# Linear attention gated by an FP4 FFN on one core: w_down's quantization, block 0's Q, GpSimd's sums and the last FFN product at other places

## The chip, the cores and the metric

The kernel runs on one core of a Trainium2 chip. The metric is the device time of one execution in microseconds (us); lower is better. Shown are the median of three runs and the span of one profiled execution, which is what the profile's rows are measured against.

## The reference

Input x is 4 sequences of 2048 tokens with D = 256 features, float32. After a layer norm the tokens go through two branches, and the second gates the first:

```python
xn = _layernorm(x)
# branch 1: linear attention (16 heads of 64), then a GELU FFN of 1024
Q = elu(xn @ Wq + bq) + 1; K = elu(xn @ Wk + bk) + 1; v = xn @ Wv + bv
KV = einsum('bshd,bshm->bhdm', K, v)
Z = 1 / (einsum('bshd,bhd->bsh', Q, K.sum(axis=1)) + 1e-6)
o = einsum('bshd,bhdm,bsh->bshm', Q, KV, Z).reshape(b, s, 1024)
x1 = _layer_norm(xn + o @ Wo + bo, g1, be1)
s = _layer_norm(x1 + gelu(x1 @ W1 + b1) @ W2 + b2, g2, be2)
# branch 2: an FFN of 704 whose inputs and weights are rounded to FP4 (E2M1) in blocks of 16
h = silu(fp4(xn) @ fp4(w_gate).T) * (fp4(xn) @ fp4(w_up).T)
g = silu(fp4(h) @ fp4(w_down).T)
out = x + s * g
```

fp4 divides each block of 16 by its largest magnitude over 6, rounds to the grid 0, 0.5, 1, 1.5, 2, 3, 4, 6, and multiplies back.

## The kernel before

**Tiling.** Tokens go in blocks of 256 (TB = 2 tiles of 128), 8 blocks to a sequence, 32 blocks in all (n = 0 to 31). Matrix products are float32; each shows as two passes (two matmul instructions) in the trace. TensorE's results go to PSUM: 4 banks of the tag mm, 2 of acc and 2 of pxk.

**Stages.** First the keys of sequence 0, in a loop of 8 rounds (n = 0 to 7): pk is the key product, ek its Exp on ScalarE, kk the elu on VectorE, pxk the sum of kk against xn. Beside them the weights are loaded, and w_gate and w_up are quantized to FP4 by quantize_gu, two chunks a round in rounds 0 to 5, in three steps (scale and division; rounding and multiplication back; transposes on TensorE, pwgu, and copies by ScalarE). Then block 0's FP4 FFN (pg is gate and up, pd the down product), and the matrix M of each half of the heads: xk copied out of PSUM, pkv, kv copied, pm (kv times Wo), in four steps of m_of_half; m_sums on GpSimd then forms the weight sums for a product in seven parts.

The main loop over blocks runs, for block n: q_of (pq, its Exp e, the elu zq), the keys of the next sequence (two subs to a block: pk, kk, pxk), sums (pz, then 1/z, stored to DRAM as z_d and read back spread over rows as zb), the FP4 values of h (qT, a product of a spread scale and a transposed grid gridT, both fetched by DMA), gate_up of block n + 1 (pg), down (pd and g), qz (zq times zb), attention (pa, added to xn, then statistics and normalization to x1), ffn_2 of block n - 1 (py), the transposes of x1 (pt_x), the scales and grids of the coming blocks, output of block n - 1 (s, o, the store), ffn_1 (pf, Gelu to hT). Block 31 has nothing beside it, and its ffn_2 runs last.

**Products in seven parts.** ffn_2, and attention for sequences 0 to 2, split both operands in halves and get from seven half-by-half products what eight give in a plain one: seven_sums makes four sums of the left operand on VectorE, w2_sums (lines 219 to 222) and m_sums (601 to 604) four of the weights on GpSimd, and add_seven puts the parts together in five VectorE additions.

**What sets the order.** Matmuls and transposes stay in program order on TensorE. VectorE and ScalarE operations do as well until in_order[0] is set to False, behind the first M products; from there a list scheduler places them by priority, with tc.issue_after as a floor. GpSimd's long operations are chained by hand through pool["last"]: gate_addend (lines 801 to 803: o = g * be2 + x, g = g * g2), ffn_addend (809, 810), attention_addend (675), and the rstd power of stats (430). Nearly all DMAs go through SyncE's queue in order. A tile's next buffer waits for its readers: x has one buffer, zq, hT, w_down and the first rows share two of tag big.

down_steps holds the two generators of quantize_down (one for each 128 rows of w_down); in block 0 their first two steps run behind the quantized x, the third (six transposes pwd, three copies) ahead of down(0, 0).

Of the kernel before, what the change touches and what calls it, by code (L numbers as in the profile page):

```python
# [22 lines left out]
def linear_attention_gated_by_fp4_ffn(  # L23
# [396 lines left out]
    def stats(x, name, js=range(TB)):  # L420

        j0, j1 = js[0], js[-1] + 1
        mv = small.tile([P, TB, 2], F32, tag="mv", name=f"mv_{name}")
        rstd = small.tile([P, TB], F32, tag="rstd", name=f"rstd_{name}")
        for j in js:
            st = small.tile([P, 6], F32, tag="st", name=f"st_{name}_{j}")
            vector.bn_stats(st, x[:, j, :])
            vector.bn_aggr(mv[:, j, :], st)
        vector.tensor_scalar(rstd[:, j0:j1], mv[:, j0:j1, 1], LN_EPS, None, ALU.add)
        pool["last"] = nc.gpsimd.tensor_tensor(  # L430
            rstd[:, j0:j1], rstd[:, j0:j1], neg_half[:, j0:j1], ALU.pow
        ).ins
        return mv, rstd
# [343 lines left out]
    def down(n, j):  # L777
        if j == 0:
            blk[n]["pd"] = acc_tile(f"pd_{n}").rearrange("p (j d) -> p j d", j=TB)
        pd = blk[n]["pd"]  # L780
        for i in range(NI):
            mm(
                pd[:, j, :], qT[:, i, j * P : (j + 1) * P], wd[:, i, :], start=i == 0, stop=i == NI - 1
            )
        if j < TB - 1:
            return
        g = work.tile([P, TB, D], F32, tag="g", name=f"g_{n}")
        scalar.activation(g, pd, AF.Silu)

        o = work.tile([P, TB, D], F32, tag="o", name=f"o_{n}")  # L790
        x = work.tile([P, TB, D], F32, tag="x", name=f"x_{n}", bufs=1)
        nc.sync.dma_start(x, rows_of(src, n))
        blk[n]["g"], blk[n]["o"], blk[n]["x"] = g, o, x

    def gate_addend(n):
        g, o, x = (blk[n][k] for k in ("g", "o", "x"))
# [10 lines left out]
            pool["last"] = nc.gpsimd.tensor_tensor(x1, x1, rows["shift"], ALU.add).ins  # L810


    def q_of(n, first=None):

        xnT = blk[n].pop("xnT")
        zq = work.tile([P, NH, T], F32, tag="big", name=f"zq_{n}")
        blk[n]["zq"] = zq
        behind = None
        for cc in range(0, NH, 2):
            pq = mm_tile(f"pq_{n}_{cc}").rearrange("p (c t) -> p c t", c=2)  # L820
            e = work.tile([P, 2, T], F32, tag="e", name=f"e_{n}_{cc}", bufs=3)
            for ci in range(2):
                c = cc + ci
                for d in range(ND):
                    mm(
                        pq[:, ci, :], wq_sb[:, d, c * P : (c + 1) * P], xnT[:, d, :],
                        start=d == 0, stop=d == ND - 1,
                    )
            scalar.activation(e, pq, AF.Exp, bias=neg_one)
            if first is not None and cc == 0:  # L830
                behind = first()
            with tc.issue_after(behind.ins) if behind is not None else nullcontext():
                vector.scalar_tensor_tensor(zq[:, cc : cc + 2, :], e, 1.0, pq, ALU.min, ALU.max)
# [93 lines left out]
    def attention(n):  # L927
        x1 = work.tile([P, TB, D], F32, tag="x1", name=f"x1_{n}")
        xn = blk[n].pop("xn")
        b = n // NB  # L930
        if in_seven(b):
            pa = [acc_tile(f"pa0_{n}"), mm_tile(f"pa1_{n}")]
            seven_products(
                pa, blk[n].pop("zs"), lambda q: m_sb[b][q], (1, 2, 4, 3, 5, 7, 6), 0, 7 * FOUR
            )
            add_seven(x1, xn, pa)
        else:
            zq = blk[n].pop("zq")
            pa = acc_tile(f"pa_{n}").rearrange("p (j d) -> p j d", j=TB)
            for j in range(TB):  # L940
                for c in range(NH):
                    mm(
                        pa[:, j, :], zq[:, c, j * P : (j + 1) * P],
                        m_sb[b, c // FOUR][:, c % FOUR, :], start=c == 0, stop=c == NH - 1,
                    )
            vector.tensor_tensor(x1, xn, pa, ALU.add)
        mv, rstd = stats(x1, f"1_{n}")
        normalize(x1, x1, mv, rstd)
        blk[n]["x1"] = x1

    def x1_T(n):
        x1 = blk[n]["x1"]
# [50 lines left out]
        seven_products(blk[n]["py"], left, w2, order, lo, to)  # L1003

    def output(n):
        g, o, x1, py = (blk[n][k] for k in ("g", "o", "x1", "py"))
        s = work.tile([P, TB, D], F32, tag="s", name=f"s_{n}", bufs=1)

        add_seven(s, x1, py)
        mv, rstd = stats(s, f"2_{n}")  # L1010
        for j in range(TB):
            vector.scalar_tensor_tensor(
                s[:, j, :], s[:, j, :], mv[:, j, 0:1], g[:, j, :], ALU.subtract, ALU.mult
            )
        for j in range(TB):
            vector.scalar_tensor_tensor(
                o[:, j, :], s[:, j, :], rstd[:, j : j + 1], o[:, j, :], ALU.mult, ALU.add
            )
        nc.sync.dma_start(rows_of(out, n), o)


    def step(gen, times=1):
# [17 lines left out]
    for n in range(NB):  # L1040
        more = n + 1 < NB
        tiles = [(f, j) for f in range(2) for j in range(TB)]
        k, kk = {}, {}

        def product(i):
            k[i] = key_product(xnT, *tiles[i], f"0_{n}_{tiles[i][0]}")

        def elu(i):
            f, j = tiles[i]
            kk[i], _ = key_elu(*k[i], f"0_{n}_{f}_{j}")  # L1050

        def onto_xn(i):
            f, j = tiles[i]
            key_xk(0, f, xn, j, kk[i], n == 0 and j == 0, not more and j == TB - 1)

        product(0)
        if more:
            st = keys_stats(n + 1)
        product(1)
        elu(0)  # L1060
        product(2)
        dep = kk[0]
        elu(1)
        if more:
            xn_next = keys_norm(n + 1, *st)
        elu(2)
        onto_xn(0)
        product(3)
        if 2 * n < 2 * I // P:
            weight = quantize_gu(range(2 * n, min(2 * n + 2, 2 * I // P)))  # L1070
        step(weight)
        for load in later.get(n, ()):
            load(dep)
        onto_xn(1)
        step(ready)
        if n < 2:
            step(constants)
        onto_xn(2)
        elu(3)
        if not more:  # L1080
            quantized_x(-1)
        if more:
            xnT = keys_xnT(n + 1, xn_next)
        step(weight)
        onto_xn(3)
        ready = weight
        if n == 5:
            add_b2(dep)
            w_down_sb = load_down()
        if n == 6:  # L1090
            load_xn(0)
            scales_x(0)
            spread_scales(-1, False, True)
            grid_of_x(0)
            grid_T(-1, NI * TB, NCH * TB)
            m_0 = m_of_half(0, 0, dep, ahead=True)
            step(m_0)
        if more:
            xn = xn_next
    load_xn(1)  # L1100
    load_xnT(0)
    down_steps = [quantize_down(w_down_sb, k) for k in range(ND)]

    step(gate, 4)
    step(m_0)
    scales_h(0, 0)
    scales_x(1)
    step(gate, 4)
    scales_h(0, 1)
    m_half = m_of_half(0, 1)  # L1110
    step(m_half)
    step(m_0, 3)
    spread_scales(0, True, True)
    in_order[0] = False
    for sub in range(2):
        keys_in(1, sub)
# [22 lines left out]
    for n in range(NBLK):  # L1139
        b, bi = divmod(n, NB)  # L1140
        subs = (2 * bi, 2 * bi + 1) if b + 1 < B else ()
        if n < last:
            gate = gate_up(n + 1)
        if n > 0:
            gate_addend(n - 1)
        if subs:
            if n > 0:
                step(m_half)
            q_of(n)
            if n == 0:  # L1150
                for sub in subs:
                    keys_T(b + 1, sub)
            load_xnT(n + 1)
            kk_ins = keys_k(b + 1, subs[0])
            block_addends(n)
            if n == 0:
                with tc.issue_after(pool["last"]):
                    w2_sums()
            with tc.issue_after(kk_ins):
                ins = quantized_x(n)  # L1160
            with tc.issue_after(sums(n, ins.ins).ins):
                for j in range(TB):
                    quantized_h(n, j)
            with tc.issue_after(ins.ins):
                for g in down_steps if n == 0 else ():
                    step(g, 2)
            if n > 0:
                keys_T(b + 1, subs[1], keys["exp"])
            step(m_half)
            keys_xk(b + 1, subs[0])  # L1170
            step(gate, 9)
            step(m_half)
            for g in down_steps if n == 0 else ():
                step(g)
            down(n, 0)
            down(n, 1)
        elif n < last:
# [28 lines left out]
        if n > 0:  # L1206
            with tc.issue_after(kk_ins):
                ffn_sums(n - 1)
            attention(n)
        if n + 2 < NBLK:  # L1210
            load_xn(n + 2)
        if subs:
# [43 lines left out]
            output(n - 1)  # L1256
        if n + 1 == last:
            q_of(last)
            ffn_1(n, range(NF // 2))
            sums(last)  # L1260
            ffn_1(n, range(NF // 2, NF))
        else:
            ffn_1(n)
        for sub in next_subs[:1]:
            keys_T(bn + 1, sub, blk[n]["gelu"])
    ffn_2(last, 4)
    ffn_sums(last)
    ffn_2(last, 28, (1, 7, 2, 4, 5, 3, 6))
    output(last)


# [32 lines left out]
```

## Time and profile before

| | us |
|---|---|
| median of three runs (lowest, highest) | 1896.48 (1895.70, 1897.93) |
| the profiled execution | 1898.94 |
| its span | 1897.2 |
| TensorE's granted clock, mean of the span | 0.996 |
| ScalarE busy, of which table loads | 706.7, 156.5 |
| DMA traffic | 187.73 MB, 99 GB/s |

Block by block: pf of block 2 starts at 316.0 us in the span and pf of block 3 at 373.8; block 30's pf starts at 1844.0, block 31's at 1875.5, and the last matmul ends at 1888.9.

An excerpt line of the views has the start, the time taken, the engine, the line and operation, the tile written and those read, and in brackets the idle time before and who ended it. L103 and L106 are the helpers that issue matmuls and transposes, L119 the one that issues VectorE and ScalarE operations, so groups are told apart by their tiles. Names ending in q (SPq, DVEq) are an engine's queue.

### The profile page before, as it was taken

The numbers are of one execution on the slowest core, as the hardware profiler recorded it, in microseconds if no ns is written. First come the engines' busy times: TensorE is split into PE (matmuls) and PEld (weight loads), VectorE is DVE, ScalarE is ACT, GpSimd is POOL, SyncE is SP. The second block draws the span as 40 slices with busy tenths as digits, with TensorE's granted clock in tenths as the row PEclk, the third lists the DMA queues.
The fourth block names the chain that finished last, engine by engine and source line by source line (L and its number), as shares of the span: only waits on it lengthen the run. The fifth ranks groups of instructions, "written<-read, shape, count | busy, mean of one in ns | idle before, by whom it ended". The sixth has DMA issues, their size and how long they took to land.

```text
span 1897.2 us, 25223 instructions
## 1 busy us (share of the span) xinstructions
PE 1864.5 (98%) x9348; PEld 1385.3 (73%) x9348; DVE 1396.8 (74%) x2530; ACT 706.7 (37%) x1191; POOL 384.0 (20%) x360
## 2 busy tenths in 40 slices
PE   9999999999999999999999999999999999999997
PEld 4456577777777777777777777777787778888876
DVE  5658777766777777777677787775777768888875
ACT  2333444334334344443233443354333333333322
POOL 1412222011121212220112230222110122222211
PEclk9999999999999999999999999999999999999999
DMA  5525655454434456644344654465442344445531
GB/s 181 191 78 112 119 105 96 108 109 89 97 66 89 113 109 121 140 74 101 83 88 78 121 99 102 92 138 105 86 89 70 70 78 87 84 89 92 91 78 43
DMA packets 228250, 187.73 MB, mean 99 GB/s; under 512 B 107655, under 2 KB 189843, under 8 KB 228126
## 3 DMA queue, kind: packets, MB, share of 16 engines
q1 hardware_dynamic: 227292, 184.53, 47.2%
q8 instruction: 74, 1.21, 0.3%
q10 hardware_dynamic: 834, 1.58, 0.3%
q14 instruction: 50, 0.41, 0.1%
HBM read 130.91 MB, written 32.59 MB: 86 GB/s over the span
## 4 chain that ended last, share of the span: by engine, by line
PE 81%; DVE 9%; DMA 6%; issue 2%; POOL 1%; ACT 1%; SPq 0%; ACTq 0%; POOLq 0%; DVEq 0%
PE pg L103 14%; PE pq L103 10%; PE pk L103 10%; PE pxk L103 10%; PE pa L103 9%; PE pf L103 9%; PE pd L103 8%; PE py L103 7%; PE pz L103 2%; POOL rstd L430 1%; DMA xn_d<-xn_k 1%; DVE x L119 1%; DMA zb<-z_d 1%; DMA xn<-xn_d 1%; DVE scale L119 1%
## 5 line engine op out<-in xcount | busy, mean ns | idle before, releaser
L430 POOL TENSOR_TENSOR rstd<-rstd,neg_half 128x2 f32<-128x2 f32 x96 | 76.8, 801 | 1352.2 <-DVE rstd L119 1039.2
L103 PE MATMUL pg<-wgu,qT 128*128 128x352 f32 x1024 | 309.2, 460 | 0.0
L103 PEld LDWEIGHTS pg<-wgu,qT 128*128 128x128 f32 x1024 | 193.8, 190 | 116.7 <-issue 14.0
L103 PE MATMUL pf<-x1T,w_sb 128*128 128x256 f32 x1024 | 229.4, 382 | 5.1 <-DVE zq L119 2.7
L103 PE MATMUL pk<-wk_sb,xnT_k 128*128 128x512 f32 x512 | 230.7, 593 | 0.8 <-ACT xnT_k L119 0.7
L103 PE MATMUL pq<-xnT,wq_sb 128*128 128x256 f32 x1024 | 226.6, 379 | 3.3 <-ACT hT L119 3.3
L103 PE MATMUL pxk<-kk,xn_k 128*128 128x512 f32 x496 | 227.6, 598 | 1.8 <-DVE kk L119 1.8
L103 PEld LDWEIGHTS pf<-x1T,w_sb 128*128 128x128 f32 x1024 | 192.8, 191 | 32.8 <-DVE zq L119 3.1
L103 PEld LDWEIGHTS pq<-xnT,wq_sb 128*128 128x128 f32 x1024 | 194.2, 190 | 30.7 <-ACT hT L119 4.4
L103 PE MATMUL pd<-wd,qT 128*128 128x256 f32 x768 | 175.2, 384 | 1.5 <-DVE qT L119 1.3
L103 PEld LDWEIGHTS pk<-wk_sb,xnT_k 128*128 128x128 f32 x512 | 96.8, 190 | 103.0 <-issue 94.5
L119 ACT ACT_TABLE_LOAD x122 | 156.5, 1283 | 40.7 <-PE pk L103 25.8
L103 PEld LDWEIGHTS pd<-wd,qT 128*128 128x128 f32 x768 | 146.9, 192 | 28.1 <-DVE qT L119 3.5
L119 ACT ACTIVATE x1T<-pt_x,bcol 128x256 f32<-128x256 f32 x64 | 32.7, 561 | 357.4 <-PE pt_x L106 357.4
L103 PEld LDWEIGHTS pxk<-kk,xn_k 128*128 128x128 f32 x496 | 89.5, 190 | 100.4 <-issue 87.0
L119 DVE SCALAR_TENSOR_TENSOR kk<-ek,pk 128x512 f32<-128x512 f32 x128 | 85.7, 685 | 99.1 <-ACT ek L119 99.1
L119 DVE TENSOR_TENSOR h<-h,pg 128x352 f32<-128x352 f32 x128 | 66.1, 516 | 100.3 <-PE pg L103 98.8
L119 ACT ACTIVATE h<-pg 128x352 f32<-128x352 f32 x128 | 58.8, 460 | 208.9 <-PE pg L103 208.9
L119 DVE SCALAR_TENSOR_TENSOR zq<-e,pq 128x512 f32<-128x512 f32 x128 | 84.2, 683 | 61.9 <-ACT e L119 61.8
L119 ACT ACTIVATE ek<-pk,neg_one 128x512 f32<-128x512 f32 x128 | 85.5, 686 | 115.8 <-PE pk L103 111.8
L103 PE MATMUL py<-w_sb,hs 128*128 128x128 f32 x1024 | 125.9, 275 | 0.0
L119 ACT ACTIVATE hT<-pf,bcol 128x256 f32<-128x256 f32 x256 | 103.8, 476 | 50.1 <-PE pf L103 49.6
(151 smaller groups left out, 2790.9 us busy)
## 6 DMA issues: line engine op xcount, KB each, us to landing
zb<-z_d SPq DMA_DIRECT2D x128, 256.0 KB, 5.9
qT<-scale_d SPq DMA_DIRECT2D x248, 128.0 KB, 5.7
x_k<-in_L_attn_src_dram SPq DMA_DIRECT2D x32, 256.0 KB
x<-in_L_attn_src_dram SPq DMA_DIRECT2D x32, 256.0 KB, 2.7
xn_d<-xn_k SPq DMA_DIRECT2D x32, 256.0 KB, 2.5
xn<-xn_d SPq DMA_DIRECT2D x32, 256.0 KB, 2.5
xnT_d<-xnT_k SPq DMA_DIRECT2D x32, 256.0 KB, 2.0
xnT<-xnT_d SPq DMA_DIRECT2D x32, 256.0 KB, 3.6
```

Source lines behind the costliest of these rows:

```text
L103: return tc.keep_in_program_order(nc.tensor.matmul(*args, **kw))
L119: ins = op(*args, **kw)
L430: pool["last"] = nc.gpsimd.tensor_tensor(rstd[:, j0:j1], rstd[:, j0:j1], neg_half[:, j0:j1], ALU.pow).ins
```

## The change

- quantize_down's steps run in rounds 6 and 7 of the first keys (its load is called in round 4 instead of 5), the last step of the second half behind the first gate product; down_steps is gone from block 0.
- Between block 0's pkv and pm: the second half's xk is copied and half of block 0's Q is computed; block 0's q_of then does the other half. The second half's M runs ahead of gate_up(1).
- attention's statistics and normalization become attention_norm, issued behind kk_ins (in blocks with keys the second sub's last kk, otherwise qz).
- GpSimd: gpsimd_behind copies one element, so that what follows in the chain waits for a tile. gate_addend(0) goes behind the first part of block 1's zq, gate_addend(30) behind block 30's last Gelu; w2_sums go from block 0 to block 1. x has two buffers (the default of its pool).
- In block 30 the z sums come after two chunks of ffn_1 instead of four.
- The last ffn_2 is a plain product: by tiles of tokens, eight products of 256 columns each, with W2 loaded whole into wk_sb; each tile has its own addition, statistics, output and store.

```diff
-        x = work.tile([P, TB, D], F32, tag="x", name=f"x_{n}", bufs=1)
+        x = work.tile([P, TB, D], F32, tag="x", name=f"x_{n}")
...
+    def gpsimd_behind(t):
+
+        one = small.tile([1, 1], F32, tag="one", name="one")
+        with tc.issue_after(pool["last"]):
+            pool["last"] = nc.gpsimd.tensor_copy(one, t[:1, 0, :1]).ins
...
-    def q_of(n, first=None):
+    def q_of(n, first=None, chunks=range(NH)):
...
-        for cc in range(0, NH, 2):
+        for cc in chunks[::2]:
...
+        blk[n]["x1"] = x1
+
+    def attention_norm(n):
+        x1 = blk[n]["x1"]
         mv, rstd = stats(x1, f"1_{n}")
         normalize(x1, x1, mv, rstd)
...
     def output(n):
...
         add_seven(s, x1, py)
-        mv, rstd = stats(s, f"2_{n}")
-        for j in range(TB):
+        output_of(n, s, range(TB))
+
+    def output_of(n, s, js):
+        g, o = blk[n]["g"], blk[n]["o"]
+        mv, rstd = stats(s, f"2_{n}_{js[0]}", js)
+        for j in js:
...
-        nc.sync.dma_start(rows_of(out, n), o)
+        j0, j1 = js[0], js[-1] + 1
+        nc.sync.dma_start(rows_of(out, n)[:, j0:j1, :], o[:, j0:j1, :])
...
             weight = quantize_gu(range(2 * n, min(2 * n + 2, 2 * I // P)))
+        else:
+            weight = quantize_down(w_down_sb, n - NB + ND)
         step(weight)
...
+        if n == 4:
+            w_down_sb = load_down()
         if n == 5:
             add_b2(dep)
-            w_down_sb = load_down()
...
-    down_steps = [quantize_down(w_down_sb, k) for k in range(ND)]
 
     step(gate, 4)
+    step(ready)
     step(m_0)
     scales_h(0, 0)
     scales_x(1)
     step(gate, 4)
     scales_h(0, 1)
+    step(m_0, 2)
     m_half = m_of_half(0, 1)
     step(m_half)
-    step(m_0, 3)
+    q_of(0, chunks=range(NH // 2))
     spread_scales(0, True, True)
+    step(m_0)
     in_order[0] = False
...
-        if n > 0:
+        if 1 < n < last:
             gate_addend(n - 1)
         if subs:
             if n > 0:
                 step(m_half)
-            q_of(n)
+            q_of(n, chunks=range(NH // 2 if n == 0 else 0, NH))
+            if n == 1:
+                gpsimd_behind(blk[n]["zq"])
+                gate_addend(n - 1)
...
-            if n == 0:
+            if n == 1:
                 with tc.issue_after(pool["last"]):
                     w2_sums()
...
-            with tc.issue_after(ins.ins):
-                for g in down_steps if n == 0 else ():
-                    step(g, 2)
...
             keys_xk(b + 1, subs[0])
+            if n == 0:
+                step(m_half)
             step(gate, 9)
             step(m_half)
-            for g in down_steps if n == 0 else ():
-                step(g)
             down(n, 0)
             down(n, 1)
...
             attention(n)
+        with tc.issue_after(kk_ins):
+            attention_norm(n)
...
             q_of(last)
-            ffn_1(n, range(NF // 2))
+            ffn_1(n, range(2))
             sums(last)
-            ffn_1(n, range(NF // 2, NF))
+            ffn_1(n, range(2, NF))
+            gpsimd_behind(blk[n]["hT"][:, NF - 1 :, :])
+            gate_addend(n)
+
+            w2_last = wk_sb.rearrange("p c (e d) -> p (c e) d", d=D)
+            nc.sync.dma_start(w2_last, by_chunks(W2))
...
-    ffn_2(last, 4)
-    ffn_sums(last)
-    ffn_2(last, 28, (1, 7, 2, 4, 5, 3, 6))
-    output(last)
+
+    py = [acc_tile("py_0"), mm_tile("py_1")]
+    for j in range(TB):
+        for c in range(NF):
+            mm(
+                py[j][:, :D], blk[last]["hT"][:, c, j * P : (j + 1) * P], w2_last[:, c, :],
+                start=c == 0, stop=c == NF - 1,
+            )
+    s = work.tile([P, TB, D], F32, tag="s", name="s_last", bufs=1)
+    for j in range(TB):
+        vector.tensor_tensor(s[:, j, :], blk[last]["x1"][:, j, :], py[j][:, :D], ALU.add)
+        output_of(last, s, (j,))
```

More of the change, by code (lines that the diff above doesn't have):

```diff
@@ L810, in ffn_addend @@
             pool["last"] = nc.gpsimd.tensor_tensor(x1, x1, rows["shift"], ALU.add).ins
-    def q_of(n, first=None):
-        xnT = blk[n].pop("xnT")
-        zq = work.tile([P, NH, T], F32, tag="big", name=f"zq_{n}")
-        blk[n]["zq"] = zq
+    def q_of(n, first=None, chunks=range(NH)):
+        xnT = blk[n]["xnT"]
+        if "zq" not in blk[n]:
+            blk[n]["zq"] = work.tile([P, NH, T], F32, tag="big", name=f"zq_{n}")
+        zq = blk[n]["zq"]
         behind = None
-        for cc in range(0, NH, 2):
+        for cc in chunks[::2]:
             pq = mm_tile(f"pq_{n}_{cc}").rearrange("p (c t) -> p c t", c=2)
@@ L946, in attention @@
             vector.tensor_tensor(x1, xn, pa, ALU.add)
+        blk[n]["x1"] = x1
+    def attention_norm(n):
+        x1 = blk[n]["x1"]
         mv, rstd = stats(x1, f"1_{n}")
         normalize(x1, x1, mv, rstd)
-        blk[n]["x1"] = x1
     def x1_T(n):
@@ L1005, in output @@
     def output(n):
-        g, o, x1, py = (blk[n][k] for k in ("g", "o", "x1", "py"))
+        x1, py = blk[n]["x1"], blk[n]["py"]
         s = work.tile([P, TB, D], F32, tag="s", name=f"s_{n}", bufs=1)
         add_seven(s, x1, py)
-        mv, rstd = stats(s, f"2_{n}")
-        for j in range(TB):
+        output_of(n, s, range(TB))
[3 more added lines that the diff above has]
+        for j in js:
             vector.scalar_tensor_tensor(
@@ L1014, in output @@
             )
-        for j in range(TB):
+        for j in js:
             vector.scalar_tensor_tensor(
```

## The prediction

> **What bounds the kernel now.** I read the page first: busy time by engine.
>
> ```profile
> span 1897.2 us, 25223 instructions
> PE 1864.5 (98%) x9348; PEld 1385.3 (73%) x9348; DVE 1396.8 (74%) x2530; ACT 706.7 (37%) x1191; POOL 384.0 (20%) x360
> ```
>
> TensorE (PE) is busy for all but 1897.2 - 1864.5 = 32.7 us. A change that keeps the number of matmul passes can win only idle PE time, time at a lowered clock, and the tail behind the last product. So the next question is where PE is idle. Busy time by stretch (stretch, its length, then busy us of PE, PEld, DVE, ACT and POOL, the granted clock, DMA share, GB/s):
>
> ```profile
> 120.00:140.00 20.00, 18.10 (x84) 10.54 (x83) 10.04 (x19) 7.17 (x13) 0.52 (x1) 1.00 0.12 24
> 140.00:160.00 20.00, 18.75 (x112) 11.97 (x110) 12.29 (x14) 11.01 (x17) 7.90 (x6) 1.00 0.88 164
> 160.00:180.00 20.00, 17.28 (x60) 11.59 (x60) 20.00 (x26) 6.30 (x14) 7.42 (x4) 0.87 0.40 105
> 180.00:200.00 20.00, 18.21 (x93) 13.26 (x93) 16.69 (x42) 3.93 (x5) 1.97 (x3) 0.96 0.10 23
> 200.00:220.00 20.00, 17.70 (x76) 13.58 (x74) 13.44 (x14) 14.76 (x27) 9.82 (x7) 1.00 0.92 155
> 220.00:240.00 20.00, 20.00 (x83) 12.87 (x82) 15.20 (x23) 5.92 (x9) 0.00 (x0) 1.00 0.44 110
> 1800.00:1850.00 50.00, 47.32 (x251) 38.10 (x249) 37.41 (x59) 15.64 (x25) 11.62 (x10) 0.97 0.42 79
> 1850.00:1897.00 47.00, 36.85 (x228) 32.83 (x220) 26.57 (x50) 9.41 (x18) 8.88 (x8) 0.94 0.17 43
> ```
>
> The holes are in block 0, from 120 to 220 us (1.90 + 1.25 + 2.72 + 1.79 + 2.30 = 9.96 us idle), and at the end. Between 340 and 1800 us only some 5 us are idle. In 160 to 180, DVE is busy for all of its 20 us: there VectorE is the bound. Third view, who PE waited for from 130 to 230 us (total, times, longest):
>
> ```profile
> PE pwd L106 <- DVE w_down L119: 2.0, 2, 1.1
> PE pm L103 <- issue: 1.9, 1, 1.9
> PE pxk L103 <- DVE kk L119: 1.8, 1, 1.8
> PE pq L103 <- ACT hT L119: 1.8, 1, 1.8
> PE pt_k L106 <- DVE zq L119: 1.2, 1, 1.2
> PE pf L103 <- ACT x1T L119: 0.5, 1, 0.5
> ```
>
> Last, the granted clock in short stretches (same columns), and two steps of the chain of waits near the end:
>
> ```profile
> 173.60:177.00 3.40, 2.00 (x9) 1.31 (x9) 3.40 (x3) 1.27 (x6) 3.24 (x3) 0.67 0.38 134
> 177.00:180.40 3.40, 3.40 (x8) 2.78 (x9) 3.40 (x3) 0.21 (x2) 3.32 (x2) 0.50 0.02 5
> 1841.00:1844.00 3.00, 0.32 (x3) 0.03 (x1) 3.00 (x4) 0.00 (x0) 2.92 (x3) 0.98 1.08 150
> 1844.00:1847.00 3.00, 3.00 (x7) 2.46 (x8) 1.71 (x3) 1.97 (x2) 0.44 (x1) 0.50 0.85 136
> ```
>
> ```profile
> 1840.43 2.88 DVE o L119 x2
> 1856.67 6.35 DMA zb<-z_d
> ```
>
> A stretch with PE mostly idle is followed by one at half clock: pd's 24 passes take 7.71 us at 176.95, against 5.18 in later blocks. Lost to the clock in block 0: 3.4 x 0.33 + 3.4 x 0.50 + 3.6 x 0.16 (180.4 to 184, clock 0.84) = 3.4 us; in the tail 3 x 0.50 + 3 x 0.05 = 1.65 us. Block 0 thus offers at most 9.96 + 3.4 = 13.4 us.
>
> **The change, part by part.**
>
> *w_down's quantization* moves from block 0 into rounds 6 and 7 of the first keys. It costs DVE per half, by its rows: first step 0.88 + 0.18 + 0.42 + 0.88 = 2.36 us, second 3 x 0.88 = 2.64; ten us in all; ACT 0.79 of Abs and about 1 of copies; PE six transposes, 0.65 by the pwgu transposes (4 in 0.44). The cover: DVE waits 2.58 us ahead of the fourth kk of round 6 (105.31 to 107.89), 2.68 ahead of that of round 7, and 5.58 us from 123.6 on. The second step of round 6 finds only 2.01 us of wait behind it, so scales, grid and the first quantized x come 0.6 us later; x is multiplied at 122.93 and its product starts at 126.56, so 2.9 us of slack take that. The 12 transposes are PE work that leaves block 0 and comes back here, net 0. Without the cover up to 2 us of PE waits appear (the 2.0 us that pwd waits for now). I take 0.2. The load of w_down starts at 24.4 us already and stays hidden.
>
> *Block 0's order.* Half of Q (16 passes, 3.46 us at 0.216 each) goes between pkv and pm, so pm's 1.9 us wait for the kv copies is filled. The price lies behind it on ScalarE and SyncE: the two Exp of Q stand ahead of scaleT's copy, pscale comes 3.46 us later on PE (1.9 of it was waiting), and Wo's second load, which waits for pm in SyncE's queue ahead of the scales' store, can hold the scales back: before, pm ended at 141.14 and the store went at 142.99; now pm ends near 144.3. Either 0.3 or 1.8 us later. The chain gridT (issue 149.30, 9.79 us) - qT (159.22) - pg (159.96) follows. M's second product (pm, 1.9 us) now runs ahead of pg and fills that wait; kv's part the same. Adding PE's work from 136.2 on: pwd 1.3 (0.65 in round 7, 0.65 behind the first tile's pg), pkv 1.15, half Q 3.46, pscale 0.27, pm 1.9, half Q 3.46, pt_k 1.26, pk 3.6, pz 1.07, pkv 1.15, pxk 3.6, pm 1.9: pg starts near 160.4 with pm done. Then pg 9.6 and pd 5.2 at full clock end at 175.4, against 184.66 before: no pwd, no m_sums or w_down operations in DVE's way. The next to be late is qz: zb lands near 173, two 1.23 us multiplications end near 175.5, so pa follows with about 0.4 us lost.
>
> *x1's norm behind the second kk* in block 0: kk no longer waits for the statistics (1.8 us of PE), but the norm then ends about 0.8 us after pxk: win 1.0. In later blocks kk already comes first (kk at 243.58, statistics at 251.85): 0.
>
> *GpSimd's sums.* w2_sums (1.93 + 1.79 + 1.45 + 1.59 = 6.76 us, at 140.7 to 148) and gate_addend(0) (3.9 us, from 201.26) go to block 1. Beside them DVE's grid took 1.84 instead of 0.89, y 1.75 instead of 0.69, xn_k 2.70 instead of 0.73, so some 3.7 us of DVE at 140 to 148 and 2 us at 201 are freed; the second lets the Gelus start 2 us earlier, and pq's wait of 1.8 goes. In block 1 GpSimd has 0.18 + 3.9 + 2.56 + 1.28 + 6.8 = 14.7 us of work behind zq's first part. zq and kk, which read PSUM, keep 0.69 beside GpSimd (271.15). It meets qT's and h's multiplications, of which only the first (222.6, needed at 224.6) has under 2 us of slack. Bounds: 0 and 5.8 us (10.7 us moved, at 3.7 lost per 6.8); I take 0.3, since w2's sums are not needed before about 253.
>
> [...]
>
> Sum for the start: 13.4 less what stays: pf's wait 0.5, the norm 0.8, qz 0.4, pt_k 0.5, the scales' delay about 1.2 = 10.0 us.
>
> *The tail.* gate_addend(30) leaves GpSimd at 1840.4, where it stretched the two o from 0.88 to 2.88; zq is free 2 us earlier, pf waits about 0.7 instead of 2.68, and the half clock behind it (1.65 us) goes. pz comes after 8 passes of pf instead of 16 and 1/x ends near 1847.4 instead of 1852.58, zb lands near 1857.8 instead of 1863.02; PE meanwhile has pf 5.2, pd 5.2 and py 1.75 and reaches pa at 1857.2, the second half of pa at 1859.1 instead of 1864.40: 5.0 us (5.3 by that sum, some kept for the two new waits). [...]
>
> The last product: 16 products of 256 columns, two passes each, 32 x 0.216 = 6.91 us, against 6.41 now (1882.46 to 1888.87). Behind it now: 1897.2 - 1888.87 = 8.3 us. Then, for the second tile: addition 0.42, statistics 0.42 + 0.17 + 0.17, power 0.87, o 0.48, store 3.0, semaphores 0.2 = 5.7. Win 8.3 - 5.7 - 0.5 = 2.1 us; the sums hs (4 x 0.69) go, but they were hidden. W2's 1 MB load in one piece has no row at its new place; SyncE is free behind wk_sb's last read, from 1504 to 1509, and w_down's load too was issued long ahead of its place in the code; cost 0 there, or, if it goes at its written place between z_d and zb, up to the 5 us that it takes at the 200 GB/s of busy stretches. I take 0.
>
> **Sum.** 10.0 + 5.0 + 2.1 - 0.3 - 0.2 = 16.6 us: span 1880.6. The profiled run lasted 1898.94, its span 1897.2; the median of the runs shown, 1896.48, lies 0.7 below the span. Forecast: 1880.
>
> **Rivals.**
> (a) *GpSimd's crowd in block 1 and the scales' store behind Wo give back part of the start.* For: DVE is busy for 15.20 of 20 us at 220 to 240, and 14.7 us of GpSimd land there. Against: PE waits for nothing there now. 5.8 + 0.6 lost: 1886.
> (b) *W2's load delays zb.* For: zb is the last wait ahead of pa. Against: nothing holds the load until then. 5 us lost: 1885.
> (c) *The change does little:* the scheduler puts the moved pieces where DVE or SyncE is late anyway, only the tail's 2.1 and half of block 0's clock loss are won: 1892.
> (d) *Slower:* the norm behind kk costs PE in every block with keys. Its place: blocks 1 to 23, where the norm's end frees pt_x. Over 0.72 us each it eats the 16.6 us; with 1.0 each, 1903. Against: kk ends 7 us ahead of the statistics there.
> (e) *More is won:* all 13.4, and 7.1 in the tail with less than 1 lost: 1876.
>
> **Chances.** Forecast (1876 to 1884) 0.58; (a) 0.14; (b) 0.10; (c) 0.07; (d) 0.05; (e) 0.06. The range leaves out most of (c), (d) and the outer half of (e): 1874.5 to 1889. A measurement of this kernel tells about 0.2% from no change, 3.8 us: faster means under 1892.7. Everything but (d) and half of (c) is faster: 0.90; same 0.05; slower 0.05.
>
> **What would show it.** Right: PE busy 19 us or more in each 20 us from 120 to 220; clock 1.00 in all of them; pd of block 0 near 5.2 us; no pwd beyond 135 us; o of block 29 near 0.88 in the tail and pf at 0.216 per pass; the last store begun about 6 us behind the last matmul. Wrong: PE waits for qT or h in block 1, a pause ahead of pg in block 0, W2's load between z_d and zb, or kk-bound pauses at every pt_x.

## The result, and the profile after

The changed kernel takes 1885.68 us, the median of four runs (1884.47 to 1888.58); the kernel before took 1897.2 us beside it (four runs, 1895.7 to 1898.35). The ratio is 0.9942, with a 95% interval of 0.9925 to 0.9959: 11.5 us are won, 0.6%. The profiled execution lasted 1884.47 us, the fastest of the four.

The page's first lines, of the changed kernel:

```profile
span 1882.7 us, 25166 instructions
PE 1860.0 (99%) x9324; PEld 1381.9 (73%) x9324; DVE 1385.3 (74%) x2524; ACT 706.3 (38%) x1191; POOL 380.8 (20%) x363
```

PE is idle for 22.7 us of the span instead of 32.7. Busy time by stretch, changed kernel, with the columns of before:

```profile
120.00:140.00 20.00, 20.00 (x98) 12.14 (x97) 13.98 (x24) 8.74 (x19) 1.27 (x1) 1.00 0.08 12
140.00:160.00 20.00, 19.52 (x116) 13.02 (x115) 12.75 (x20) 10.49 (x19) 0.53 (x1) 1.00 0.88 192
160.00:180.00 20.00, 18.32 (x85) 13.86 (x83) 13.61 (x22) 5.45 (x9) 5.19 (x4) 1.00 0.44 105
180.00:200.00 20.00, 18.33 (x84) 12.86 (x85) 13.99 (x38) 9.92 (x19) 2.08 (x3) 1.00 0.25 74
200.00:220.00 20.00, 18.18 (x76) 11.31 (x76) 9.03 (x11) 10.99 (x16) 10.61 (x9) 1.00 0.89 151
220.00:240.00 20.00, 20.00 (x98) 15.03 (x97) 17.94 (x28) 5.22 (x8) 3.68 (x3) 1.00 0.33 63
1800.00:1850.00 50.00, 49.29 (x274) 40.33 (x267) 33.42 (x56) 15.35 (x27) 7.99 (x8) 1.00 0.38 79
```

DVE is busy for 13.61 of 20 us in 160 to 180 where it was full, and the clock is 1.00 in every stretch. From 120 to 220 PE is idle for 5.65 us (0.48 + 1.68 + 1.67 + 1.82) instead of 9.96. The view of who PE waited for, 130 to 230 us, changed kernel:

```profile
PE pk L103 <- DVE zq L119: 1.8, 1, 1.8
PE pa L103 <- DVE zs L119: 1.6, 1, 1.6
PE pxk L103 <- DVE kk L119: 1.1, 1, 1.1
PE pf L103 <- ACT x1T L119: 0.5, 1, 0.5
PE pk L103 <- ACT xnT_k L119: 0.4, 1, 0.4
```

The waits of pwd, pm, pq and pt_k are gone; pk, which had none, and pa now wait. The chain of waits near the end (start, length, what), to be held against o's 2.88 and zb at 1856.67 before:

```profile
1833.21 0.88 DVE o L119 x2
1834.09 0.61 DVE zq L119
1834.70 0.04 issue
1834.74 1.99 PE pf L103 x8
1836.74 1.00 PE pz L103 x16
1837.74 5.38 PE pf L103 x24
...
1870.02 3.47 PE py L103 x16
```

The two o of block 29 are back at 0.88 us, pz follows 8 passes of pf, and zb is no longer in the chain.

**Where the time came from.** Two marks cut the span in three: block 1's first pf and block 29's first pf. The first comes at 251.88 instead of 259.52 (7.64 us won), the stretch between them takes 1531.2 us against 1531.1 before (nothing), and the rest takes 99.6 instead of 106.6 (7.0 won). That makes 14.5, which is the difference of the two profiled spans (1897.2 and 1882.7), and 3 us more than that of the medians: the profiled execution of before (1898.94) lay above its median, that of the changed kernel was its fastest.

### The profile page after: what moved, and what is told of

The parts are those of the page before. It is cut to its first block, busy times and chain, and to the rows that moved or that the text cites. A ratio compares the mean times of both kernels' runs of the same rounds, so it can differ in the third digit from the quotient of the medians.

```text
span 1882.7 us, 25166 instructions
## 1 busy us (share of the span) xinstructions
PE 1860.0 (99%) x9324; PEld 1381.9 (73%) x9324; DVE 1385.3 (74%) x2524; ACT 706.3 (38%) x1191; POOL 380.8 (20%) x363
## 4 chain that ended last, share of the span: by engine, by line
PE 79%; DVE 9%; DMA 7%; ACT 2%; issue 1%; POOL 1%; SPq 1%; ACTq 0%; POOLq 0%; DVEq 0%
PE pg L103 14%; PE pk L103 11%; PE pq L103 10%; PE pxk L103 10%; PE pf L103 9%; PE pa L103 8%; PE pd L103 8%; PE py L103 6%; DMA zb<-z_d 2%; PE pz L103 2%; POOL rstd L430 1%; DVE x L119 1%; DMA xn_d<-xn_k 1%; DMA xn<-xn_d 1%; DVE hs L119 1%
## 5 line engine op out<-in xcount | busy, mean ns | idle before, releaser
L430 POOL TENSOR_TENSOR rstd<-rstd,neg_half 128x2 f32<-128x2 f32 (+1 forms) x97 | 77.5, 799 | 1322.6 <-DVE rstd L119 995.8
L119 ACT ACTIVATE x1T<-pt_x,bcol 128x256 f32<-128x256 f32 x64 | 32.7, 561 | 355.4 <-PE pt_x L106 355.4
L119 DVE TENSOR_TENSOR h<-h,pg 128x352 f32<-128x352 f32 x128 | 66.2, 517 | 99.8 <-PE pg L103 96.9
L119 DVE TENSOR_TENSOR zq<-zq,zb 128x1024 f32<-128x1024 f32 x64 | 79.2, 1238 | 64.5 <-DMA zb<-z_d 64.4
```

The source lines that it names most:

```text
L119: ins = op(*args, **kw)
L430: pool["last"] = nc.gpsimd.tensor_tensor(rstd[:, j0:j1], rstd[:, j0:j1], neg_half[:, j0:j1], ALU.pow).ins
```

## The experiments

Each was timed in turns with the kernel before (medians 1898.39, 1897.74 and 1897.09 in three series, each on another chip), five runs or more of each. For the start I use the time from block 0's first pg to block 1's first pf, which leaves out when qT's transfers happen to land; for the tail the time from block 29's first pf to the end.

| kernel | pg | pf of block 1 | between | tail | time | ratio to before, 95% interval |
|---|---|---|---|---|---|---|
| before | 159.96 | 259.52 | 99.6 | 106.6 | | 1 |
| changed | 160.53 | 251.88 | 91.4 | 99.6 | 1885.68 | 0.9942 (0.9925 to 0.9959) |
| e0_after | 161.34 | 251.83 | 90.5 | 99.5 | 1887.25 | 0.9937 (0.9925 to 0.9950) |
| e1_wdown_alone | 162.32 | 255.59 | 93.3 | 107.3 | 1895.00 | 0.9976 (0.9964 to 0.9987) |
| e2_wdown_back | 159.10 | 256.73 | 97.6 | 100.0 | 1892.80 | 0.9976 (0.9966 to 0.9986) |
| e3_tail_seven | 160.64 | 250.38 | 89.7 | 101.7 | 1889.52 | 0.9951 (0.9938 to 0.9963) |
| e4_gate30_back | 162.05 | 253.67 | 91.6 | 101.6 | 1890.48 | 0.9962 (0.9950 to 0.9975) |
| e5_order_back | 161.90 | 255.08 | 93.2 | 100.2 | 1890.66 | 0.9964 (0.9952 to 0.9977) |
| e6_sums_back | 161.70 | 260.64 | 98.9 | 99.8 | 1896.08 | 0.9988 (0.9979 to 0.9997) |
| e7_norm_back | 161.77 | 250.31 | 88.5 | 99.4 | 1885.99 | 0.9940 (0.9928 to 0.9952) |
| e8_three_waits | 160.87 | 250.90 | 90.0 | 99.7 | 1885.05 | 0.9934 (0.9922 to 0.9947) |
| e9_scales_behind_kk | 161.41 | 249.85 | 88.4 | 99.7 | 1885.78 | 0.9938 (0.9926 to 0.9950) |
| e10_gate0_top | 160.46 | 259.98 | 99.5 | 99.5 | 1894.15 | 0.9983 (0.9974 to 0.9991) |
| e11_w2sums_block0 | 161.19 | 251.55 | 90.4 | 99.4 | 1887.22 | 0.9947 (0.9935 to 0.9959) |

**e0_after**: the changed kernel again, as the base of the others.

> The changed kernel itself, a second time, on the chip of the next three. Its four runs so far spread from 1884.5 to 1888.6 us, the kernel before from 1895.7 to 1898.4. If the spread is of single runs, this median lies at 1885 to 1887 and the ratio at 0.993 to 0.995; if the fastest run (1884.5) is the rule on some chips, the median lies under 1885.

The tail repeats within 0.1 us, and the kernels below that keep this tail have 99.4 to 100.2. The start is less steady: it takes 91.4 and 90.5 us here, and 89.7 and 91.6 in e3 and e4, whose edits lie in the tail; block 1's pf comes at 250.38 and 253.67 in those two. The span of this profile is 1885.5, since the middle took 1534.2 us, 3 us more; the largest single part is 1.2 us between the first pf of blocks 16 and 17 (58.32 instead of 57.09). Differences of medians below some 3 us, and of starts below some 2 us, therefore mean little here.

**e1_wdown_alone**: the kernel before with w_down's quantization in rounds 6 and 7, and nothing else of the change.

```
+        else:
+            weight = quantize_down(w_down_sb, n - NB + ND)
...
+        if n == 4:
+            w_down_sb = load_down()
...
-    down_steps = [quantize_down(w_down_sb, k) for k in range(ND)]
```

> The kernel before with one part of the change: w_down's quantization beside the keys. If VectorE's ten us of w_down were what held block 0 (theory), pg still starts near 160 us, but pd starts near 172.5 instead of 177.0 at full clock, and the run is 4 to 6 us faster than the kernel before. If the fills on TensorE (Q ahead of M's product) are what counts (rival), pd is held by the same DMA chain and by m_sums, and the run is under 2 us faster.

The interval between the marks falls by 6.3 us, but block 1's pf comes only 3.9 us earlier and the median falls by 3.4, between the two expectations: pg waits 2.7 us for qT, the clock of 160 to 180 is 0.91, and pd starts at 175.13. Freed DVE time was not yet freed PE time. In this kernel the loads that spread qT's scales stand behind the grid's transposing DMA in SyncE's queue and are issued at 150.04 instead of 145.33, and the product that makes qT starts at 161.57 instead of 159.22.

**e2_wdown_back**: the changed kernel with this one move undone.

```
-        else:
-            weight = quantize_down(w_down_sb, n - NB + ND)
...
+    down_steps = [quantize_down(w_down_sb, k) for k in range(ND)]
...
+            for g in down_steps if n == 0 else ():
+                step(g)
```

> The changed kernel with w_down's quantization back in block 0, all else kept. Theory: VectorE is again busy without a gap from 160 to 180, pd starts 4 us or more later and TensorE's clock drops: 4 to 6 us slower than the changed kernel. Rival: under 2 us slower.

Busy time by stretch, of this kernel, and who PE waited for:

```profile
160.00:180.00 20.00, 14.84 (x49) 9.75 (x48) 20.00 (x28) 6.21 (x13) 6.22 (x4) 0.83 0.36 88
```

```profile
PE pwd L106 <- DVE w_down L119: 2.6, 1, 2.6
PE pg L103 <- DVE h L119: 1.8, 1, 1.8
```

DVE is full again (20.00 of 20) and PE falls to 14.84 at clock 0.83. So VectorE was the bound of that stretch, and this move took it away: 6.3 us between the marks, as the only part or as the last.

**e3_tail_seven**: the last product in seven parts again.

```
-    py = [acc_tile("py_0"), mm_tile("py_1")]
...
+    ffn_2(last, 4)
+    ffn_sums(last)
+    ffn_2(last, 28, (1, 7, 2, 4, 5, 3, 6))
+    output(last)
```

> The changed kernel with the last FFN product in seven parts, as before. Theory: from the last matmul to the end 8.3 us instead of 5.7, and 0.5 us less of matmuls: 2 us slower than the changed kernel. Rival: the store ends the run either way and the two stores of half size cost what the pipelining wins: no difference.

From block 31's pf to the end it takes 22.0 us (1867.41 to 1889.4) against 19.8 in e0_after: 2.2 us, against 2.1 in the prediction.

**e4_gate30_back**: gate_addend(30) at the top of block 31 again.

```
-        if 1 < n < last:
+        if n > 1:
...
-            gpsimd_behind(blk[n]["hT"][:, NF - 1 :, :])
-            gate_addend(n)
```

> The changed kernel with gate_addend(30) back at the top of block 31, where nothing holds it behind block 30's last Gelu. Theory: GpSimd runs it at the same moment as the two o of block 29, these take 2.9 us instead of 0.9, pf waits 2.7 us instead of 0.7 and the next 3 us run at half clock: 3 to 4.5 us slower than the changed kernel. Rival: only the 2 us shift, the clock stays at 1.00: 2 us slower.

The timeline of this kernel (start, length, engine, operation, idle time before and its releaser), and its granted clock behind that wait:

```profile
1836.76 2.88 DVE L119 SCALAR_TENSOR_TENSOR o<-s,rstd,o 128x256 f32<-128x256 f32 x2 [0.59 <-POOL rstd L430]
...
1840.30 1.99 PE L103 MATMUL pf<-x1T,w_sb 128*128 128x256 f32 x8 [2.68 <-DVE zq L119]
```

```profile
1840.00:1843.00 3.00, 2.70 (x24) 1.85 (x24) 2.04 (x4) 2.63 (x4) 0.77 (x1) 1.00 0.90 147
1843.00:1846.00 3.00, 3.00 (x21) 2.47 (x14) 2.60 (x3) 0.92 (x3) 0.00 (x0) 1.00 0.00 0
```

The stretched o and the wait of 2.68 us come back to the digit, and the tail grows by 2.1 us. The half clock does not come back: here the same idle time leaves the clock at 1.00, as the rival of the expectation had it. The rest of this profile's longer span lies in the start (1.8 us later at block 1's pf) and the middle (2.0), which the edit leaves as they are.

**e5_order_back**: Q of block 0 in one piece behind M's product again.

```
-    step(m_0, 2)
     m_half = m_of_half(0, 1)
     step(m_half)
-    q_of(0, chunks=range(NH // 2))
+    step(m_0, 3)
     spread_scales(0, True, True)
-    step(m_0)
```

> The changed kernel with the order of block 0's Q and M as before (all of Q behind M's first product, the second half of M's product behind gate_up). Theory: pm waits 1.9 us for kv again and pm's second 1.9 us stand between pg and pd, while pg's start is held by gridT near 160 us: 2 to 3.5 us slower than the changed kernel. Rival: block 0 is held by the DMA chain and qz, and the order of TensorE's work is worth under 1 us.

pm waits again, and the clock behind it falls (timeline of PE in this kernel):

```profile
140.73 3.52 PE L103 MATMUL pm<-wo,kv 128*128 128x256 f32 x8 [1.90 <-issue]
```

The wait is 1.9 us and the half clock costs 1.6 (3.52 instead of 1.89 us for the eight passes), but pg starts only 0.6 us later than in e0_after, since the second half of M's product has left its place ahead of pg. Behind pg that product takes 1.7 us and pa waits 0.9 for m_sums, together close to the 2.7 us more between the marks, and block 1's pf comes 3.2 us later than in e0_after.

**e6_sums_back**: block 0's gate_addend and w2_sums at their old places.

```
-        if 1 < n < last:
+        if 0 < n < last:
...
-                gpsimd_behind(blk[n]["zq"])
-                gate_addend(n - 1)
...
-            if n == 1:
+            if n == 0:
                 with tc.issue_after(pool["last"]):
                     w2_sums()
```

> The changed kernel with w2_sums back in block 0 and gate_addend(0) back at block 1's top. Theory: VectorE's grids at 140 to 148 take twice as long, but gridT is issued behind the scales' DMAs anyway (under 0.5 us); xn_k at 195 takes 2 us more, so Gelu and the transposed keys come later: 1 to 3 us slower than the changed kernel. Rival: the crowd of GpSimd work that the change makes in block 1 costs more than that, and this kernel is the faster one.

This was far off: 8.8 us instead of 1 to 3. Two smaller runs split it.

**e10_gate0_top**: gate_addend(0) alone back at the top of block 1 (the first two hunks of e6).

> The changed kernel with block 0's gate_addend alone back at the top of block 1, so that GpSimd's sums (it, ffn_addend and attention_addend, all in one chain) run at once beside VectorE's xn_k and grids; w2_sums stay in block 1. Theory (the 8.8 us that block 1's pf came later with both moves undone stem from here: xn_k 2.69 instead of 0.73 us, grids near 2 instead of 0.9, so gridT's transposing DMA at 206.6 instead of 198.2, the keys' one behind it, and xnT_k's copy 6.5 us later, which stands ahead of e on ScalarE): the pk of block 1 waits 4.5 us or more longer than in the changed kernel, pf at 256.5 or later, time 5 to 8 us above. Rival (w2_sums in block 0 was the main part): pf within 2 us of 251.8 and the time within 2 us.

The timeline of this kernel, all engines:

```profile
194.26 1.27 POOL L807 TENSOR_TENSOR o<-g,be_r 128x512 f32<-128x512 f32 x1
194.33 2.70 DVE L119 TENSOR_SCALAR xn_k<-x_k,mv,rstd 128x256 f32<-128x256 f32 x2 [0.81 <-POOL rstd L430]
...
196.95 1.96 DVE L119 SCALAR_TENSOR_TENSOR h<-m_h,h 128x704 f32<-128x704 bf16 x1
...
205.30 1.37 SPq L737 DMA_TRANSPOSE gridT<-grid  x1
206.77 1.40 SPq L516 DMA_TRANSPOSE apartT<-apart  x1
...
210.07 1.33 ACT L119 COPY xnT_k<-apartT 128x1024 uint16<-128x1024 uint16 x1 [7.50 <-DMA apartT<-apart]
211.42 1.28 ACT L119 ACT_TABLE_LOAD   x1
212.71 2.42 ACT L119 ACTIVATE e<-pq,neg_one 128x512 f32<-128x512 f32 x4
...
214.18 6.77 PE L103 MATMUL pk<-wk_sb,xnT_k 128*128 128x512 f32 x8 [7.20 <-DVE zq L119]
```

And the same part of the changed kernel:

```profile
198.32 1.38 SPq L737 DMA_TRANSPOSE gridT<-grid  x1
...
199.78 1.39 SPq L516 DMA_TRANSPOSE apartT<-apart  x1
...
205.03 1.34 ACT L119 COPY xnT_k<-apartT 128x1024 uint16<-128x1024 uint16 x1 [3.44 <-DMA apartT<-apart]
...
209.14 3.70 PE L103 MATMUL pk<-wk_sb,xnT_k 128*128 128x512 f32 x8 [1.82 <-DVE zq L119]
```

Read downwards, it is one chain over five engines. GpSimd's long sums stretch DVE's xn_k (0.73 to 2.70) and the steps to the grid (0.89 to 1.96); the grid's transposing DMA goes 7.0 us later; the keys' one stands behind it in SyncE's queue; the copy of the transposed keys waits for that, and Q's Exp stands behind the copy on ScalarE. So pk waits 7.20 us instead of 1.82, and then runs at half clock (0.50 from 213 to 220 us), 6.77 instead of 3.70: 5.4 + 3.1 = 8.5, and 8.2 show between the marks.

The changed kernel's own 1.82 us are another matter. In e3, e4 and e11 the order of SyncE's queue is the same, and block 1's pk doesn't wait for zq. The timeline of e4_gate30_back:

```profile
200.50 1.38 SPq L737 DMA_TRANSPOSE gridT<-grid  x1
...
201.97 1.36 SPq L516 DMA_TRANSPOSE apartT<-apart  x1
...
205.26 1.34 ACT L119 COPY xnT_k<-apartT 128x1024 uint16<-128x1024 uint16 x1 [1.48 <-DMA apartT<-apart]
...
209.37 3.70 PE L103 MATMUL pk<-wk_sb,xnT_k 128*128 128x512 f32 x8
```

The copy starts 3.3 us behind the issue of the keys' transposing DMA here, 3.2 in e3, 3.4 in e11 and 3.3 in e10, but 5.3 in the changed kernel and in e0_after. Against e3 the chain of e10 closes at every step: grid 6.8 us later, copy 6.9, pk 6.9. So the old place of gate_addend costs what e10 shows, and the new place leaves a wait at pk only where this DMA lands late; why it does so in two of these six profiles no run shows.

In the kernel before, the keys' transposing DMA was issued ahead of the grid's (205.94 and 215.39), and beside the same GpSimd sums the only wait there was pq's 1.75 us. So the old place seems to have become expensive by the scheduler's new order in SyncE's queue; no run changes that order alone.

**e11_w2sums_block0**: w2_sums alone back in block 0 (the last hunk of e6).

> The changed kernel with w2_sums alone back in block 0 (four sums on GpSimd, 6.3 us beside VectorE's scales and grids there). Theory: gridT's transposing DMA and block 0's products come 0.5 to 2 us later, pf of block 1 0.5 to 2.5 us later than 251.8, time 0.5 to 2.5 us above the changed kernel's, and with the run that has only the gate's part back the two make up the 9 us of both. Rival (w2_sums is the main part): 5 us or more. Second rival: they hide, within 0.5 us.

90.4 us between the marks, as in e0_after: 6.9 us of GpSimd there make DVE's last grid step 1.9 us later (148.74 instead of 146.84), and that hides. All of e6 is gate_addend's place.

**e7_norm_back**: x1's statistics and norm inside attention again, with no floor behind kk.

```
         blk[n]["x1"] = x1
-
-    def attention_norm(n):
-        x1 = blk[n]["x1"]
         mv, rstd = stats(x1, f"1_{n}")
         normalize(x1, x1, mv, rstd)
...
-        with tc.issue_after(kk_ins):
-            attention_norm(n)
```

> The changed kernel with x1's statistics and norm back inside the attention, so that VectorE is free to put them ahead of the keys' kk, in every block. Theory (the prediction's step, a gain of 1.0 us in block 0 from kk going first): in block 0 the keys' second product waits 1 to 2 us longer for kk than the 1.1 us of the changed kernel, block 1's first pf comes 1 to 2 us later than 251.8, and the time is 1 to 2 us above the changed kernel's. Rival (the order is the same either way, since kk is ready long before): no difference, within 0.5 us, the same order of VectorE's instructions. Second rival (the prediction's fourth one, turned round: norm behind kk costs something in each later block): the time falls by 1 us or more.

pxk waits 1.3 us instead of 1.1: the move is worth 0.2 us. The expected 1 to 2 us didn't come. The marks lie even closer (88.5), 1.2 us below e3's; in this kernel the keys' transposing DMA goes first again (196.65, the grid's at 205.77), and pk doesn't wait. What the order and what the spread of the start has in it is not told apart.

**e8_three_waits**: the three waits that the changed kernel has left, each treated by an edit of its order: qz and its sums ahead of h's rounding in block 0, the copy of the transposed keys behind block 1's first Exp, Exp's table loaded early by a one-element Exp.

```
+            with tc.issue_after(act.ins):
+                scalar.activation(early, neg_one[:1, :1], AF.Exp)
...
+                keys_T(b + 1, subs[0], blk[n - 1]["gelu"])
                 gpsimd_behind(blk[n]["zq"])
...
-            with tc.issue_after(qz_ins) if not subs else nullcontext():
+            with tc.issue_after(sums_ins if n == 0 else qz_ins) if not subs or n == 0 else nullcontext():
                 scales_h(n + 1, 1)
```

> The changed kernel with three more edits for the waits left in blocks 0 and 1: h's rounding and the second scale behind qz and the sums (pa's wait of 1.6 us), the copy of the transposed keys behind block 1's first Exps (pk's wait of 1.8 us), a one-element Exp behind block 0's g, so that the table is there when pk ends (pxk's wait of 1.1 us). Theory: these are what the start did not win; 3 to 4.5 us faster than the changed kernel. Rival: TensorE only waits a little later, for the scales and grids of block 2 (pg behind qT): under 1 us faster.

pa waits 0.2 us and pk no longer at all (as in e3, e4 and e11 without any edit of it), 3 us in sum, but block 1's pf comes only 1.0 us earlier. The timeline of this kernel says who took the rest:

```profile
185.75 0.69 DVE L119 TENSOR_REDUCE scale<-xn 128x32 f32<-128x512 f32 x1 [1.11 <-DMA xn<-xn_d]
...
187.16 0.63 DVE L119 SCALAR_TENSOR_TENSOR kk<-ek,pk 128x512 f32<-128x512 f32 x1
...
187.84 5.40 PE L103 MATMUL pxk<-kk,xn_k 128*128 128x512 f32 x8 [1.96 <-DVE kk L119]
```

ek had ended at 184.95, but DVE stood at the scales of block 2 and waited for xn's load, with kk queued behind it; pxk then waited 1.96 us and ran at a lowered clock, 5.40 instead of 3.70.

**e9_scales_behind_kk**: e8, and those scales behind kk.

```
+                with tc.issue_after(kk_ins) if n == 0 else nullcontext():
+                    scales_x(n + 2)
```

> The kernel with the three waits taken away, and block 2's scale reduction of xn placed behind the keys' kk in block 0, since it waited 1.11 us there for xn's load and kk stood behind it (pxk's wait of 1.96 and its half clock, 5.40 us instead of 3.70). Theory: pxk begins with no wait or below 0.5 us near 186 and takes 3.7 us; the norm's end is then next (pt_x near 190.5 to 191.7 instead of 193.1); block 1's first pf comes at 248.5 to 249.5 instead of 250.9, and the time is 1.5 to 3 us below the changed kernel's. Rival (the chain of VectorE from pa to the norm sets pt_x, whichever of its parts goes first): pt_x within 0.5 us of 193.1, pf at 250.5 or later, time within 1 us of the changed kernel's.

The timeline of this kernel:

```profile
182.39 3.60 PE L103 MATMUL pk<-wk_sb,xnT_k 128*128 128x512 f32 x8
...
185.83 3.70 PE L103 MATMUL pxk<-kk,xn_k 128*128 128x512 f32 x8
...
190.56 0.87 PE L106 MATMUL pt_x<-ident,x 128*128 128x128 f32 x4 [1.03 <-DVE x L119]
```

pxk follows pk without a pause, and the norm is next to be late, by 1.03 us at pt_x. Between the marks 2.9 us are won against the changed kernel; pg began 0.9 later, which leaves 2.0 at block 1's pf, and the profiled span is 1881.3. Against e3, the shortest start of the unedited ones, it is 1.3 us. The medians don't show it (1885.78 against 1885.68 and 1887.25): it is less than the middle varies by. No kernel tried is shown to beat the changed one.

## Why the prediction was right, and where its sizes were off

It forecast 1880 with a range of 1874.5 to 1889, faster at 0.90. The kernel is faster, at 1885.68, inside the range and 5.7 us above the forecast. That is outside the 1876 to 1884 that it gave 0.58, and near rival (a)'s 1886, but this rival's mechanism is not what cost the time: PE is busy 20.00 of 20 us in 220 to 240, beside GpSimd's sums, and the scales were stored at 143.68 us, ahead of Wo's load. The parts of the change did what the prediction said of them, with the exceptions below; that the time landed on a rival's number is chance.

- **w_down** behaved as written: cover in rounds 6 and 7 (PE without a pause from 100 to 140 us), DVE's full stretch gone, pd at 169.99 for 5.34 us. pd ended at 175.33, predicted 175.4 (its own terms, 160.4 + 9.6 + 5.2, make 175.2); pg began at 160.53, predicted 160.4.
- **Block 0's order** filled pm's wait; undone in e5 it costs 3.2 us. That is more than the kernel before lost there: its pm ran at full clock behind the same 1.90 us (139.17, 1.97 us for the eight passes), while e5's ran at half. The failed step is "about 0.4 us lost" at pa: it was 1.55. DVE put 2.3 us of h's rounding, product and grid between the two multiplications of qz, and e8, which puts the rounding and grid behind them, has 0.2 (timeline of the changed kernel):

```profile
171.91 1.23 DVE L119 TENSOR_TENSOR zq<-zq,zb 128x1024 f32<-128x1024 f32 x1 [2.89 <-DMA zb<-z_d]
173.05 0.88 DVE L119 SCALAR_TENSOR_TENSOR h<-m_h,h 128x704 f32<-128x704 bf16 x1
173.85 0.51 DVE L119 TENSOR_TENSOR h<-h,pg 128x352 f32<-128x352 f32 x1
174.28 0.88 DVE L119 SCALAR_TENSOR_TENSOR grid<-m_h,h 128x704 bf16<-128x704 bf16 x1
175.08 1.22 DVE L119 TENSOR_TENSOR zq<-zq,zb 128x1024 f32<-128x1024 f32 x1
```

- **The norm behind kk**, "win 1.0", is worth 0.2 by e7; "the norm then ends about 0.8 us after pxk" did not happen either. The wait of 1.1 us that pxk keeps is Exp's: a table load of 1.28 us stands between pk's product and ek. In e1, with the norm at its old place, pxk waits the same 1.1 us instead of the 1.8 of before, so emptying DVE had already taken what this step was to win. The rival of a slower kernel from this move, (d), falls with it.
- **GpSimd's sums**: cost 0 in block 1 (0.3 predicted) in this profile. Beside them the two steps that make qT took 1.47 and 3.07 us instead of 0.69 and 1.76. Where pk doesn't wait ahead of it this can show: in e4 and e9 the first step took 1.81 and 1.72 us, and pg started 0.1 us behind its end, after pauses of 1.34 and 0.96. The step that failed is "pq's wait of 1.8 goes". It went, and came back at pk, 1.82 us: ScalarE, which used to be late with the Gelus, was now late with Q's Exp, behind the copy of the transposed keys. In e3, e4 and e11, where the keys' transposing DMA landed 2 us sooner, it did not come back, so this part of the shortfall is one of single executions. The prediction followed the freed time to the next instruction and not through SyncE's queue to the one behind it. So it took the move for a small term; with the rest of the change in place it is the largest, 8.2 us (e10).
- **The start as a whole**: 10.0 predicted, 7.6 measured. By the prediction's own ceiling: 9.96 idle less 5.65 that stay, plus 3.4 of half clock, is 7.7. The 2.4 missing are pa's 1.2 too much and pk's 1.8, less 0.6 on smaller terms.
- **The tail**: 7.1 predicted, 7.0 measured; 2.2 of it from the plain product (e3, 2.1 predicted), 2.1 from gate_addend's place (e4), and by subtraction 2.7 for pz after 8 passes and for the half clock. That last pair was not told apart by a run. The step that tied 1.65 us of half clock to pf's wait holds in the kernel before and in e1 (2.67 us, then 5.41 us for 16 passes of pf, against 3.72 for the next 16) and not in e4 (2.68 us, then a clock of 1.00). W2's load cost nothing: it was issued at 1497.2 us, behind wk_sb's last read.
- **From span to time**: the prediction put the median 0.6 us below the predicted span. The changed kernel's median lies 3.0 above its profiled span: both profiled executions took 1.7 to 1.8 us more than their spans, and this one was 1.2 below its median. That the median of before lay under the profiled span was chance, since the profiled run of before was 2.5 above that median. This is 3.6 of the 5.7 us; the other 2.1 are the start's 2.4 and the tail's 0.1, less the 0.3 and 0.2 that were set aside for block 1 and the keys and not needed (0.1 is rounding).

The parts don't add up. Undoing them one by one costs 6.3 (e2), 1.8 (e5) and 8.2 us (e10) between the marks, 16.3 in sum, where the whole change won 8.2 there; at block 1's pf it is 4.9, 3.2 and 8.1, against 7.6. Each part's worth was measured with the others in place. This fits stalls that cover one another, so that PE waits once where two of them are open; no run undid two parts to show it.

## What to carry to other kernels

When a stall is removed, follow the freed instruction through every in-order queue to the next thing that stands behind it, the DMA queue included: here a GpSimd sum delayed a product of TensorE by way of VectorE, SyncE's queue and ScalarE, and pk waited 7.20 us instead of 1.82 (e10). An engine full for a whole stretch is worth emptying, but what that yields shows only once the queues beside it are in order too: in e1 the interval between the marks fell by 6.3 us and block 1's pf came 3.9 earlier. And compare stretches between fixed marks of the program before medians, where single executions differ by as much as the gain that you look for; then see how well a stretch repeats in kernels that leave it as it is.

## What the runs showed of the hardware

**Waits of 1.90 to 2.68 us were followed by a lower clock in some profiles and not in others.** A wait of 2.68 us was followed by a clock of 0.50 (1844 to 1847) in the kernel before, and by 1.00 (1840 to 1846) in e4; behind one of 2.67 us in e1, 16 passes of pf took 5.41 us and the next 16 took 3.72. Behind a wait of 1.96 us in e8 a product took 5.40 us instead of 3.70, with a mean clock of 0.79 from 186 to 190 us and 0.78 from 190 to 194. One of 1.90 us was followed by passes at half speed in e5 (3.52 us for eight), and by passes at full speed at pm in the kernel before (1.97 us for eight) and at pk in e0_after (3.70 us, as behind the 1.82 us of the changed kernel). Around the end of the 7.20 us in e10 the clock was 0.50, from 213 to 220 us. What decides whether the clock falls behind a wait is not shown.

**A table load can stand in the path or ahead of it.** In the changed kernel the load before the first Exp of block 0's second keys started at 185.60, as pk's product arrived, with ScalarE idle for 9.63 us ahead of it. In the kernel before, the load for the same Exp ran at 185.99, and the Exp waited for pk until 192.67. In e8 a one-element Exp behind the Silu of block 0 had the table loaded at 176.34, and ek came 1.3 us earlier against pk than in the changed kernel. What sets the moment of the load is not shown.

**GpSimd slowed VectorE by operation, not evenly.** Beside its sums xn_k took 2.70 instead of 0.73 us and a grid step 1.96 instead of 0.89 (e10, at 194.33 and 196.95). But in the changed kernel zq and h times pg, which read PSUM, kept their 0.6 and 0.5 us (208.40, 221.29), and a reduction of h, which reads no PSUM, kept its 0.89 us (222.87) beside the sum of 222.57 to 223.84.
